# Moving the gather selections behind the column-tiled evictions, and trimming an image's last step

## The chip, the cores and the metric

The kernel runs on one core of a Trainium2 chip. Its engines work side by side, each through its own list of instructions in order: TensorE (PE) multiplies matrices into PSUM, VectorE (DVE) and ScalarE (ACT) do elementwise work and bring PSUM results to SBUF, GpSimd (POOL) mostly issues DMAs here, and SyncE (SP) issues some more. The metric is the time of one launch in microseconds (us), the median of several runs. Lower is better.

## The reference

The input is x of 8 images, 32 channels, 128 x 128 pixels, f32. After a group normalisation, layer 0 finds for each pixel the 8 best of 25 offsets in a 5 x 5 window (smallest sum of squared differences over a 3 x 3 patch and all channels) and gathers the 8 shifted copies into 256 channels, xb. Then:

```python
dct = _conv(xb, dct_w, groups=C)
h = jax.nn.relu(_conv(_conv(xb, w1), w2, groups=CK, pad=1))
h = jax.nn.relu(_conv(_conv(h, w3), w4, groups=CK, pad=1))
wiener = jax.nn.sigmoid(_conv(_conv(h, w5), w6, groups=CK, pad=1))
filt = _conv(wiener * dct, inv_dct_w, groups=C)
return _conv(filt, agg_w)
```

Each of w1, w3, w5 is a 1x1 convolution of 256 to 256 channels, and each of w2, w4, w6 a depthwise 3x3. The result is added to x. Layer 1 normalises again, applies one 5x5 kernel to all channels, and adds.

## The kernel before

**Steps and slots.** An image is cut into 16 blocks of 8 rows (NS = 16), and the main loop runs over 8 x 17 = 136 steps: the 17th step of an image (n == NS) only finishes the rows that still lack a neighbour below. Because each 3x3 convolution needs a row below, the second 1x1/3x3 pair works one row behind, the third two rows and the end three rows behind; so in the last step pair i has only i rows to give. Each step has four slots, for i in (3, 2, 1, 0). Slot i = 3, 2, 1 does the i-th pair of convolutions, for a block that is i - 1 steps old; slot 0 does the end (the DCT product, the aggregation) for a block two steps old. In each slot one unit (4 rows, 4 of the 8 copies) of a coming block is gathered.

**Two halves of the channels.** The upper 128 output channels of a pair go the V way: `pointwise_v` (L627 to L645) multiplies on PE into PSUM tiles pv, ACT copies them to tv, and `depthwise_v` (L674) starts the 3x3 with one ACT scale copy (L685), lets DVE add the other eight taps (L688), and ends with an activation on ACT ("dv", L692). The lower 128 go the T way: `pointwise_t` (L647) multiplies with the PE array split into four column groups of 32, so that the four groups hold the rows r, r + 4 of a block; the PSUM tile p holds them, ACT copies it to t (L667), and two DMAs on SP (L670, L672) bring the rows below and above into other partitions of t. `depthwise_t` (L696) does the 3x3 as matmuls from t into pw (L709), in a group of u = 0, 1, three dx and four j; with f32 each is two instructions, so 48 in a group. Two ACT activations (L721) bring pw to SBUF. The depthwise group of slot i is issued one slot later: "`next(dt)`", ahead of the gather in slot 0, behind it in the other slots. Its pw tiles have one buffer for each u.

**The gather.** `gather_load` (L548) issues on POOL the DMAs that bring pixel rows (xt) and, broadcast to all partitions, index rows (ib). `gather_select` (L578) makes on ACT, for each of two ib tiles, a Square with the partition's number as bias and a Relu (L584, L585), which leave 1 where the index fits and 0 elsewhere: the selection sel. `gather_pixels` (L588) multiplies xt with sel on PE (pg, L599), and ACT copies pg to xb (L606). In a slot, pixels of unit u, the selection of unit u + 1, and the load of unit u + 3 are issued.

**Work of the next image.** In between, the search for the best offsets of the next image and layer 1 of the last one are cut into small tasks that wait in four queues: "D" on DVE, "A" on ACT, "P" and "Q" on PE. A task has a cost in us, and may have a due time in ticks. `tick` (L886) grants each slot a credit, and runs D tasks for that credit. For the search a pair of difference tiles df is made on DVE (L410), squared on ACT at `run("A")` (L418), and summed on PE into pd at the next slot's `run("Q")` (L425). Other tasks transpose (px, pt, pi) or apply layer 1's 5x5 (p5, the line L836), at `run("P")`.

**What sets the order.** PE, DVE and ACT run in exactly the order of the program (`manual_schedule(engines=ORDERED)`). The DMA queues of POOL and SP are ordered by the framework. The PSUM tiles pv, p, pg, pc, pa, px, pt, pi, p5 share one pool ps_x of five buffers. In a slot the order is: pv and its copies, the scale copy; the last step's end (`later`, with pa); P tasks; in slot 0 the DCT product pc; Q tasks; the selection of u + 1 and the load of u + 3; the tick; DVE's taps; p with its copies to t; in slot 0 the depthwise group of slot 1; the pixels of u; in the other slots the depthwise group of the slot before; A tasks; then for the slot before dv and the activations of pw.

Of the kernel before, what the change touches and what calls it, by code (L numbers as in the profile page):

```python
# [17 lines left out]
C, K, H, W = 32, 8, 128, 128  # L18
CK = C * K
NO = 25  # L20
R = 8
NS = H // R
# [21 lines left out]
def bm3d_conv_preact(  # L44
# [16 lines left out]
    nc = tc.nc  # L61
# [85 lines left out]
    with tc.tile_pool(name="setup", bufs=1) as sp, tc.tile_pool(  # L147
# [23 lines left out]
        for name, w in (("w1", w1), ("w3", w3), ("w5", w5)):  # L171
            t = sp.tile([P, 2, CK], F32, name=f"nat_{name}", tag=f"nat_{name}")
            nc.sync.dma_start(t, w.rearrange("(m p) i a b -> p m (i a b)", p=P))
            if name == "w1":

                nat, t = t, sp.tile([P, 2, CK], F32, name="w1_kc")
# [6 lines left out]
        for name, dst in (("w1", lw1), ("w3", lw3), ("w5", lw5)):  # L183
            for g in range(2):
                ps = spp.tile([P, CK], F32, name=f"ps_{name}_{g}", tag="ps")
# [434 lines left out]
    def rows_before_v(i, b, n):  # L620
        v = tv[i - 1]
        if n < NS:
            nc.sync.dma_start(v[:, 0:2], v[:, R : R + 2])
        else:
            nc.gpsimd.memset(v[:, 0 : i + 1], 0.0)
# [21 lines left out]
    def pointwise_t(i, b, n, lhsT, src):  # L647
        t = tb[i - 1]
        nb = 2 if n < NS else 1
        if n == NS and i == 1:  # L650
            nc.gpsimd.memset(t[:, :, 2], 0.0)
        else:
            for q in range(2):
                ps = ps_x.tile([P, 2, 2, W], F32, name=f"p{i}_{b}_{n}_{q}", tag="x")
                for e in range(2):
                    s = slice(C * (2 * q + e), C * (2 * q + e + 1))
                    for g in range(2):
                        rows = src(g)
                        for r in range(4):
                            nc.tensor.matmul(  # L660
                                ps[C * r : C * (r + 1), e, :nb],
                                lhsT[:, g, s],
                                rows[:, r : r + 4 * nb - 3 : 4],
                                start=g == 0,
                                stop=g == 1,
                            )
                nc.scalar.copy(t[:, 2 * q : 2 * q + 2, 2 : 2 + nb], ps[:, :, :nb])  # L667
            for r in range(i - 1) if n == 0 else range(i - 1, 4) if n == NS else ():
                nc.gpsimd.memset(t[C * r : C * (r + 1), :, 2], 0.0)
        nc.sync.dma_start(t[64:P, :, 0:nb], t[0:64, :, 2 : 2 + nb])  # L670
        if nb == 2:
            nc.sync.dma_start(t[0:64, :, 1], t[64:P, :, 2])  # L672

    def depthwise_v(i, b, n):  # L674
        v = tv[i - 1]
        nr = R if n < NS else 4
        out_ = accp.tile([P, R, W], F32, name=f"acc{i}_{b}_{n}_1", tag=f"acc{i}1")
        acc = out_[:, :nr]
        for k, (dy, dx) in enumerate(
            ((1, 1), (0, 0), (0, 1), (0, 2), (1, 0), (1, 2), (2, 0), (2, 1), (2, 2))  # L680
        ):
            tap = dwv[:, i - 1, 3 * dy + dx : 3 * dy + dx + 1]
            rows = v[:, dy : dy + nr, dx : dx + W]
            if k == 0:
                nc.scalar.activation(acc, rows, AF.Copy, scale=tap)  # L685
                yield out_
            else:
                nc.vector.scalar_tensor_tensor(  # L688
                    acc, rows, tap, acc, op0=ALU.mult, op1=ALU.add
                )  # L690
        yield
        nc.scalar.activation(acc, acc, funcs[i - 1])  # L692
        yield
        rows_before_v(i, b, n)

    def depthwise_t(i, b, n):  # L696
        t = tb[i - 1].rearrange("p q (h k) w -> p q h k w", k=2)
        nb = 2 if n < NS else 1

        pt = [  # L700
            ps_dw.tile([P, 2, 2, W], F32, name=f"pw{i}_{b}_{n}_{u}", tag=f"dw{u}")
            for u in range(2)
        ]
        for u in range(2):
            hi = 96 if u == 0 else P
            for dx in (0, -1, 1):
                xa, xz = max(0, -dx), min(W, W - dx)
                for j in range(4):
                    nc.tensor.matmul(  # L709
                        pt[u][C * j : C * (j + 1), :, :nb, xa:xz],  # L710
                        dwd[0:hi, i - 1, u, j, dx + 1],
                        t[0:hi, j, :, :nb, xa + dx : xz + dx],
                        start=dx == 0,
                        stop=True,
                        skip_group_check=True,
                    )
        yield 1
        acc = accp.tile([P, R, W], F32, name=f"acc{i}_{b}_{n}_0", tag=f"acc{i}0")
        rows = acc.rearrange("p (k e) w -> p e k w", e=4)
        for u in range(2):  # L720
            nc.scalar.activation(rows[:, u:4:2, :nb], pt[u][:, :, :nb], funcs[i - 1])  # L721
        rows_before_t(i, b, n)
        accs[i, b, n][0] = acc

# [139 lines left out]
    lws, funcs = (lw1, lw3, lw5), (AF.Relu, AF.Relu, AF.Sigmoid)  # L864
    accs, fins = {}, {}

    def unit(stage, u):
        if 0 <= u < len(units) and units[u]:
            if stage is gather_load:
                at = (units[u][0], units[u][1] % 8 // 2)  # L870
                until(lambda: at in ready, 4.0)
            stage(*units[u])
# [28 lines left out]
    with tc.manual_schedule(engines=ORDERED):  # L901
        push(prep(0))
        push(mixes())
        xbd[0] = dram.tile([P, 2, H, W], F32, name="xbd_0", tag="xbd")
        for i in range(3):
            nc.gpsimd.memset(tb[i][0:64, :, 0], 0.0)
        for u in range(7):
            unit(gather_load, u)
            unit(gather_select, u - 2)
            unit(gather_pixels, u - 3)  # L910
        u = 4

        dt = dv = kept = iter(())

        later = lambda: None

        for s in range(len(steps) + 2):
            if s < len(steps):
                b, n = steps[s]
                if s == 2:  # L920
                    push(bands())
                if n == (0 if b else 4) and b + 1 < NB:
                    until(lambda: b in ready, 4.0)
                    push(prep(b + 1))
                if n == NS - 1 and b + 1 < NB:
                    until(lambda: b + 1 in ready, 4.0)
                    xbd[b + 1] = dram.tile([P, 2, H, W], F32, name=f"xbd_{b+1}", tag="xbd")
            for i in (3, 2, 1, 0):
                si = s - (i - 1 if i else 2)
                live = 0 <= si < len(steps)  # L930
                new_v = new_t = iter(())
                if live:
                    bi, ni = steps[si]

                if live and i:
                    src = source(i, bi, ni)
                    pointwise_v(i, bi, ni, lws[i - 1], src)
                    new_v, new_t = depthwise_v(i, bi, ni), depthwise_t(i, bi, ni)
                    accs[i, bi, ni] = [None, next(new_v)]
                later()  # L940
                later = lambda: None
                if live and not i:
                    if ni == 0:
                        x1d[bi] = dram.tile([C, H, W], F32, name=f"x1d_{bi}", tag="x1d")
                        stats[bi] = work.tile([P, NS + 1, 6], F32, name=f"stat_{bi}", tag="stat")
                    xr, xf, j0, j1 = fins.pop(si)
                run("P")
                if live and not i:
                    final_dct(bi, ni, accs[3, bi, ni], xf, j0, j1)

                run("Q")
                if s < len(steps):
                    unit(gather_select, u + 1)
                    unit(gather_load, u + 3)
                    tick(b, i)
                next(new_v, None)
                if live and i:
                    pointwise_t(i, bi, ni, lws[i - 1], src)
                next(kept, None)
                if not i:  # L960
                    next(dt, None)
                if s < len(steps):
                    unit(gather_pixels, u)
                    u += 1
                if i:
                    next(dt, None)
                run("A")
                next(dv, None)
                next(dt, None)
                kept, dv, dt = dv, new_v, new_t  # L970
                if live and not i:
                    later = partial(end, bi, ni, xr, j0, j1)
                if not i and 0 <= s - 1 < len(steps):
                    fins[s - 1] = final_load(*steps[s - 1])
        next(kept, None)
        later()
        until(lambda: NB - 1 in done, 4.0)
# [62 lines left out]
```

## Time and profile before

| | |
|---|---|
| median of 3 runs | 7131.84 us (7118.07 to 7140.6) |
| the profiled execution | 7131.18 us |
| its span, first to last instruction | 7129.4 us |
| mean granted clock of PE | 0.978 |
| PE busy | 6700.9 us, 94% |
| DVE busy | 5840.1 us, 82% |
| ACT busy | 5061.7 us, 71% |
| of it the selections (L584, L585) | 1165.4 + 1084.4 us, 1024 each |
| the t copies (L667) | 423.0 us, 800 |
| POOL busy | 2738.3 us, 38% |

Busy is the time in which an engine executes; the share is that of the span. A row of the waits reads: who waited, for whose result, total us, times, longest. A row of the timeline reads: start and length in us from the span's start, engine, line, operation, output and inputs, shapes, and how many instructions are merged; the bracket gives the idle time before it and what ended it. A row of the windows reads: the stretch, its length, then the busy us and instructions of PE, PE's weight loads, DVE, ACT and POOL, then PE's granted clock (1.00 is full), the DMA engines' share and GB/s. The clock row of the page gives the granted clock in tenths of full speed in 40 slices. PE's ends are modelled, so its busy time is an upper view.

### The profile page before, as it was taken

Reading aid. Unit: us, or ns where it says so; the run is one execution under the profiler, and the core shown is the slowest. Engines: PE = TensorE matmul, PEld = TensorE weight load, DVE = VectorE, ACT = ScalarE, POOL = GpSimd, SP = SyncE. Lnnn points to the kernel's source line nnn. Section 1 sums busy time; section 2 is a strip of 40 time slices with the busy share of each in tenths; the row PEclk is TensorE's granted clock in tenths of the full one; section 3 lists DMA queues with packets and bytes.
Section 4 is the critical chain, followed back from the end, with each engine's and each line's share of the span. In section 5 each row is a group of like instructions: output and inputs, shape, how many; then the busy total and the mean of one; then the engine's idle time right before and its main releaser. Section 6 shows DMA issues by size and latency. Waiting matters only on the chain. (4 is left out here: it accounts for less than half of the span.)

```text
span 7129.4 us, 229485 instructions
## 1 busy us (share of the span) xinstructions
PE 6700.9 (94%) x100226; PEld 3166.8 (44%) x100226; DVE 5840.1 (82%) x8606; ACT 5061.7 (71%) x6706; POOL 2738.3 (38%) x4599
## 2 busy tenths in 40 slices
PE   4699999999999999999999999999999999999997
PEld 1344444444444444444444444444444444444443
DVE  6689978888888898878888898888978889767675
ACT  4687768677686777867677776877768677666762
POOL 6244336333353343533335343543335333232222
PEclk8899999999999999999999999999999999999999
DMA  3566756666565575666656666566656666555652
GB/s 81 130 145 151 155 129 153 142 148 149 134 156 143 138 166 125 160 145 145 154 127 160 141 152 140 142 161 150 152 130 150 151 145 147 125 146 139 149 134 63
DMA packets 765484, 1007.70 MB, mean 141 GB/s; under 512 B 215008, under 2 KB 578592, under 8 KB 764480
## 3 DMA queue, kind: packets, MB, share of 16 engines
q0 software_dynamic: 378400, 733.67, 42.5%
q1 hardware_dynamic: 381056, 256.86, 17.0%
q8 instruction: 788, 12.91, 0.8%
q10 hardware_dynamic: 5024, 2.49, 0.2%
q14 instruction: 216, 1.77, 0.1%
HBM read 542.24 MB, written 217.01 MB: 106 GB/s over the span
## 5 line engine op out<-in xcount | busy, mean ns | idle before, releaser
L688 DVE SCALAR_TENSOR_TENSOR acc<-tv,dwv,acc 128x1024 f32<-128x1024 f32 (+1 forms) x3264 | 4084.0, 1253 | 223.1 <-ACT acc L685 109.5
L709 PE MATMUL pw<-t,dwd 128*32 128x508 f32 (+6 forms) x19584 | 2179.5, 592 | 156.8 <-DMA t<-t 109.4
L709 PEld LDWEIGHTS pw<-t,dwd 128*32 128x32 f32 (+1 forms) x19584 | 702.3, 111 | 1393.8 <-issue 1205.9
L570 POOL DMA_DIRECT2D ib<-idxd x1024 | 575.2, 563 | 1881.5 <-ACT sel L585 1764.8
L584 ACT ACTIVATE ib<-ib,nplace 128x1024 bf16<-128x1024 bf16 x1024 | 1165.4, 1138 | 25.6 <-DMA ib<-idxd 25.6
L585 ACT ACTIVATE sel<-ib 128x1024 f32<-128x1024 bf16 x1024 | 1084.4, 1059 | 32.6
L660 PE MATMUL p<-acc,lw 128*32 128x256 f32 x17408 | 994.1, 375 | 10.3 <-issue 10.0
L637 PE MATMUL pv<-acc,lw 128*128 128x512 f32 (+1 forms) x2112 | 971.9, 602 | 10.5 <-DVE acc L760 6.3
L606 ACT COPY xb<-pg 128x512 f32<-128x512 f32 x512 | 303.6, 593 | 713.5 <-PE pg L599 713.1
L645 ACT COPY tv<-pv 128x512 f32<-128x512 f32 (+2 forms) x784 | 444.8, 584 | 482.0 <-PE pv L637 463.6
L660 PEld LDWEIGHTS p<-acc,lw 128*32 128x32 f32 x17408 | 562.8, 110 | 429.6 <-issue 81.0
L721 ACT ACTIVATE acc<-pw 128x512 f32<-128x512 f32 (+1 forms) x816 | 452.8, 584 | 341.2 <-PE pw L709 340.8
L599 PEld LDWEIGHTS pg<-sel,xt 128*32 128x32 f32 x45056 | 591.2, 111 | 225.7 <-issue 126.1
L599 PE MATMUL pg<-sel,xt 128*32 128x48 f32 x45056 | 593.6, 206 | 82.9 <-issue 53.1
L780 DVE TENSOR_TENSOR xr<-xr,pa 128x256 f32<-128x256 f32 (+2 forms) x136 | 55.1, 405 | 717.9 <-PE pa L773 698.8
L637 PEld LDWEIGHTS pv<-acc,lw 128*128 128x128 f32 x2112 | 381.0, 191 | 407.7 <-issue 376.7
L410 DVE TENSOR_TENSOR df<-xn 128x786 f32<-128x786 f32 (+2 forms) x576 | 529.0, 969 | 17.2 <-PE pd L425 14.6
L667 ACT COPY t<-p 128x512 f32<-128x512 f32 x800 | 423.0, 570 | 119.8 <-PE p L660 116.5
L418 ACT ACTIVATE df<-df 128x786 f32<-128x786 f32 (+2 forms) x576 | 461.1, 862 | 50.4 <-DVE df L410 49.3
L685 ACT ACTIVATE acc<-tv,dwv 128x1024 f32<-128x1024 f32 (+1 forms) x408 | 459.8, 1127 | 45.8 <-PE pa L773 32.1
L637 PE MATMUL pv<-xb,lw 128*128 128x512 f32 x1024 | 475.7, 607 | 0.0
L757 PE MATMUL pc<-xf,ldct 128*128 128x512 f32 (+2 forms) x1056 | 470.9, 588 | 0.0
(128 smaller groups left out, 6397.3 us busy)
## 6 DMA issues: line engine op xcount, KB each, us to landing
ib<-idxd POOLq DMA_DIRECT2D x1024, 256.0 KB
xbd<-xb POOLq DMA_DIRECT2D x128, 1024.0 KB
xf<-xbd POOLq DMA_DIRECT2D x480, 256.0 KB
t<-t SPq DMA_DIRECT2D x792, 128.0 KB, 4.8
t<-t SPq DMA_DIRECT2D x384, 256.0 KB, 4.9
tv<-tv SPq DMA_DIRECT2D x384, 130.0 KB, 4.1
xt<-xtd POOLq DMA_DIRECT2D x240, 176.0 KB
xl<-xs POOLq DMA_DIRECT2D x256, 64.0 KB
```

The source lines that it names most:

```text
L410: nc.vector.tensor_sub(df[:, :, ca:cz], xn[:, r0 : r0 + SR, ca:cz], xn[:, r0 + dy : r0 + dy + SR, ca + dx : cz + dx],)
L418: nc.scalar.activation(df[:, :, ca:cz], df[:, :, ca:cz], AF.Square)
L570: nc.gpsimd.dma_start(ib.rearrange("p k y x -> p (k y x)"), idxd[b][s4 // 8, s4 % 8, 4 * k0 : 4 * k0 + 8] .rearrange("k x -> (k x)") .part ...
L584: nc.scalar.activation(ib, ib, AF.Square, bias=nplace)
L585: nc.scalar.activation(sel, ib, AF.Relu, scale=-1.0, bias=1.0)
L599: nc.tensor.matmul(pg[C * j : C * (j + 1), :, xa:xz], xt[:, t], sels[j // 2][:, j % 2, :, xa:xz], start=True, stop=True,)
L637: nc.tensor.matmul(ps[:, :hr], lhsT[:, g, P:CK], src(g)[:, h : h + hr], start=g == 0, stop=g == 1,)
L660: nc.tensor.matmul(ps[C * r : C * (r + 1), e, :nb], lhsT[:, g, s], rows[:, r : r + 4 * nb - 3 : 4], start=g == 0, stop=g == 1,)
L685: nc.scalar.activation(acc, rows, AF.Copy, scale=tap)
L688: nc.vector.scalar_tensor_tensor(acc, rows, tap, acc, op0=ALU.mult, op1=ALU.add)
L709: nc.tensor.matmul(pt[u][C * j : C * (j + 1), :, :nb, xa:xz], dwd[0:hi, i - 1, u, j, dx + 1], t[0:hi, j, :, :nb, xa + dx : xz + dx], start ...
L757: nc.tensor.matmul(ps[:, : z - a], ldct[:, m], xf[:, m, a:z], start=True, stop=True)
```

## The change

Two things are done. First, in the main loop `gather_select` of unit u + 1 and `gather_load` of unit u + 3 move from ahead of the tick to behind `gather_pixels` of unit u. On ACT the selections thus stand behind the copies to t and the copy to xb, and ahead of the A tasks, dv and the activations of pw. The load's DMAs on POOL move behind those of the tick.

Second, in an image's last step (n == NS) `pointwise_t` multiplies and copies only i - 1 rows where it did 4 (for i = 1 it did none already), `depthwise_v` works on i rows where it did 4, and `depthwise_t` on as many rows of each u as lie among the i that count: 1 and 0 for i = 1, 1 and 1 for i = 2, 2 and 1 for i = 3, where it did 2 and 2.

```diff
 def pointwise_t(i, b, n, lhsT, src):
+        nr = 4 if n < NS else i - 1
-                        for r in range(4):
+                        for r in range(nr):
...
-                nc.scalar.copy(t[:, 2 * q : 2 * q + 2, 2 : 2 + nb], ps[:, :, :nb])
+                nc.scalar.copy(
+                    t[: C * nr, 2 * q : 2 * q + 2, 2 : 2 + nb], ps[: C * nr, :, :nb]
+                )
 def depthwise_v(i, b, n):
-        nr = R if n < NS else 4
+        nr = R if n < NS else i
 def depthwise_t(i, b, n):
+        nh = [2 if n < NS else (i + 1 - u) // 2 for u in range(2)]
-                for j in range(4):
+                for j in range(4 if nh[u] else 0):
                     nc.tensor.matmul(
-                        pt[u][C * j : C * (j + 1), :, :nb, xa:xz],
+                        pt[u][C * j : C * (j + 1), : nh[u], :nb, xa:xz],
                         dwd[0:hi, i - 1, u, j, dx + 1],
-                        t[0:hi, j, :, :nb, xa + dx : xz + dx],
+                        t[0:hi, j, : nh[u], :nb, xa + dx : xz + dx],
...
-            nc.scalar.activation(rows[:, u:4:2, :nb], pt[u][:, :, :nb], funcs[i - 1])
+            if nh[u]:
+                nc.scalar.activation(
+                    rows[:, u : u + 2 * nh[u] - 1 : 2, :nb], pt[u][:, : nh[u], :nb], funcs[i - 1]
+                )
 main loop, each slot
                 run("Q")
                 if s < len(steps):
-                    unit(gather_select, u + 1)
-                    unit(gather_load, u + 3)
                     tick(b, i)
...
                 if s < len(steps):
                     unit(gather_pixels, u)
+                    unit(gather_select, u + 1)
+                    unit(gather_load, u + 3)
                     u += 1
                 if i:
                     next(dt, None)
                 run("A")
```

## The prediction

> **What bounds the kernel now.** I read the page first, for the engines' totals and the clock row. TensorE (PE) is busy 94% of the span and no other engine comes near it:
>
> ```profile
> PE 6700.9 (94%) x100226; PEld 3166.8 (44%) x100226; DVE 5840.1 (82%) x8606; ACT 5061.7 (71%) x6706; POOL 2738.3 (38%) x4599
> PEclk8899999999999999999999999999999999999999
> ```
>
> The question is therefore which waits are left on PE, and what else could put new ones there. Second view, PE's waits:
>
> ```profile
> PE pw L709 <- DMA t<-t: 109.4, 53, 12.1
> PE pg L599 <- issue: 53.1, 36, 4.7
> ...
> PE pd L425 <- ACT df L418: 29.5, 29, 2.9
> PE pw L709 <- issue: 27.2, 16, 5.4
> ```
>
> Of some 430 us idle (span less busy) a good part lies before 300 us, in the start. In the body the largest single wait is the depthwise matmuls (pw) waiting for the row copies of t. Third view, ScalarE's (ACT) waits: it has much idle time, and most of it is spent before the pixel copy xb.
>
> ```profile
> ACT xb L606 <- PE pg L599: 713.1, 179, 13.4
> ACT tv L645 <- PE pv L637: 463.6, 439, 3.2
> ```
>
> Fourth view, the timeline of ACT and then PE in one ordinary slot (i = 2, behind slot 3):
>
> ```profile
> 3109.81 0.59 ACT L606 COPY xb<-pg 128x512 f32<-128x512 f32 x1 [0.33 <-PE pg L599]
> 3110.29 1.60 ACT L418 ACTIVATE df<-df 128x786 f32<-128x786 f32 x2
> 3111.79 0.57 ACT L645 COPY tv<-pv 128x512 f32<-128x512 f32 x1
> 3113.40 0.59 ACT L645 COPY tv<-pv 128x512 f32<-128x512 f32 x1 [1.04 <-PE pv L637]
> 3114.02 1.15 ACT L685 ACTIVATE acc<-tv,dwv 128x1024 f32<-128x1024 f32 x1
> 3115.08 1.13 ACT L584 ACTIVATE ib<-ib,nplace 128x1024 bf16<-128x1024 bf16 x1
> 3116.24 1.06 ACT L585 ACTIVATE sel<-ib 128x1024 f32<-128x1024 bf16 x1
> 3117.21 1.13 ACT L584 ACTIVATE ib<-ib,nplace 128x1024 bf16<-128x1024 bf16 x1
> 3118.37 1.06 ACT L585 ACTIVATE sel<-ib 128x1024 f32<-128x1024 bf16 x1
> 3119.34 1.05 ACT L667 COPY t<-p 128x512 f32<-128x512 f32 x2
> ```
>
> ```profile
> 3109.66 3.70 PE L637 MATMUL pv<-acc,lw 128*128 128x512 f32 x8
> 3113.30 0.86 PE L425 MATMUL pd<-df,neg 128*32 128x393 f32 x8
> 3113.98 3.63 PE L660 MATMUL p<-acc,lw 128*32 128x256 f32 x64
> ...
> 3118.80 1.49 PE L709 MATMUL pw<-t,dwd 96*32 96x512 f32 x12 [0.28 <-DMA t<-t]
> ```
>
> Two things are to be seen. PE finished p at 3117.6, but its eviction to t starts only at 3119.34, behind four selection instructions that take 3119.34 - 3115.08 = 4.26 us. And the squares of df run right behind xb and end at 3111.9, 1.4 us before PE wants them for pd at 3113.30. The first is what the moved block relieves. The second is what it is put in front of.
>
> Last, the windows view shows what a PE wait costs beyond itself: the stretch from 3087.50 to 3091.00 follows a 2.29 us wait for t, and its granted clock is 0.56.
>
> ```profile
> 3087.50:3091.00 3.50, 3.45 (x20) 1.25 (x24) 3.36 (x18) 0.00 (x0) 1.31 (x2) 0.56 0.07 20
> 3091.00:3094.50 3.50, 3.50 (x45) 1.22 (x40) 0.05 (x1) 0.00 (x0) 0.89 (x2) 0.95 0.32 86
> ```
>
> The 48 matmuls there spread over 7.03 us against 5.33 elsewhere: 1.70 us more, half of a 3.41 us stretch at half clock. In the body (300 to 7040 us) half-clock stretches followed 1 of 59 PE waits under 1.6 us, 7 of 24 between 1.6 and 2.2, 16 of 25 between 2.2 and 3, and 11 of 11 above 3.
>
> **The change part by part.** The sum is made against the profiled execution: 7131.18 us, a span of 7129.4 and 1.8 around it; the median of the runs is 7131.84, so either may stand as base.
>
> *t earlier (gain).* With the selections gone from before them, the t copies start as soon as p and the scale copy (L685) are done. By the timeline, the end of p to the end of t is usually 3.0 to 3.4 us; without the queue about 1. I went through the depthwise groups that waited after 300 us: 122.5 us of first waits, and of each I count no more than what its t copy lay behind p less 1.0 us. That gives 97 us; the rest are waits that the earlier copy doesn't reach. In 24 of these groups the half clock cost a further 46 us, of which I take 38. Bounds: nothing, if the landing is set by shared DMA queues (from 2.4 to 14.2 us, median 4.9), to all 168. SP's order stays; each t copy's two DMAs only start earlier on it.
>
> *Squares later (loss).* Behind xb the order becomes selections, squares, dv activation, pw evictions, and next slot's pv copies. In the slot shown: pg's end 3109.66, first selection 0.63 later, 4.26 of selections, 1.60 of squares, and about 0.45 for the second half of pd: pd would end 6.98 us behind pg where it ended 4.5. PE loses 2.5 us. The same step for all 184 places where squares follow an xb copy (0.75 us per further square, so that four squares end 8.0 us behind pg): between slots 3 and 2 PE has only pv before pd, and 31 of 42 are late, 58 us in all; between slots 0 and 3 it has pv and pa, 47 of 66 are late, 89 us; where a 5.33 us depthwise group lies between, 6 of 76, 2 us. Sum 150 us. It can be half, if PE would have waited there for something else; nothing in the wait table is large enough to absorb all.
>
> *Clock (loss).* The delays counted are 32 under 1.6 us, 15 up to 2.2, 31 up to 3 and 6 above. By the shares above, 15 x 7/24 + 31 x 16/25 + 6 = 30 half-clock stretches of 1.71 us: 52 us. Bounds 0 to 84 x 1.71 = 144. The Trainium skill, "TensorE: Matmul & The Clock Gate" (the section on HAM oscillation), asks only that PE have no gaps above about 3.4 us; by that rule nearly all of these delays would be free of a clock loss, and the sum below would come out about 50 us lower. The trace disagrees: 23 of its 49 body waits between 1.6 and 3 us were followed by half clock, so the row decides.
>
> *PSUM buffers (loss).* ps_x has five buffers, and pv of slot 3 is now evicted some 7.4 us behind pg(0): 0.66 + 4.26 + 0.95 (dv) + 0.95 (pw) + 0.6. In 7 slots 3 with pi and no pd, PE wants the first one back at 3.7 + 1.07 + 0.4 = 5.2 us: 2.2 x 7 = 15 us. Elsewhere p or p5 fills the time. Bounds 0 to 30.
>
> *Short slots (loss).* A selection is now done 4.92 us behind pg, and the next pg wants it. Ordinary slots have pv 3.70 and p 3.66 between. At an image's end slot 2 has pv of 0.7 and p of 1.95, slot 3 pv 1.13, pa 1.07, p 1.9: 2.0 and 0.8 us missing, once per image, less some waits already there: 20 us. Bounds 0 to 25.
>
> *VectorE (loss).* Taps of slot 3 wait for a scale copy now 9.0 us behind pg(0); DVE otherwise gets there at about 7.7. DVE has 699 us idle waiting for pa, which covers it except in the steps full of max searches: 10 us, bounds 0 to 40. If that cover were gone it would be 1.3 us in each of 136 steps, 177.
>
> *Gather loads (0).* POOL's ib load is freed by the selection and so starts later, but is wanted two slots later: about 15 us, as before. POOL's work of the tick now stands ahead of it. POOL already waits 1764.8 us for sel in front of ib, so its rank matters little. ACT waited 25.6 us for ib; bounds -25 to 25.
>
> *Last step.* A short depthwise group takes 2.79 us (48 matmuls of 256 columns). Rows left: half of the columns and half of the groups for i = 1 (0.7 us), half the columns for i = 2 (1.4), three quarters for i = 3 (2.1): 4.2 us an image, 33 us gained, bounds 15 to 33. pointwise_t issues 16 or 32 instead of 64, but the four row groups ran side by side, so their time is that of one group: 16 x 0.11 = 1.8 us, nothing gained. A single row may lose the overlap of weight loads: the nearest row is pc at 128 columns, 5.1 us for 32, 0.16 each, so +0.8 us in 8 slots: 6 us, bounds 0 to 13. VectorE's eight taps shrink from 0.75 us each, covered by the same 699 us idle; ACT's two activations likewise, by its 713 us before xb.
>
> Sum: 150 + 52 + 15 + 20 + 10 + 6 = 253 lost, 97 + 38 + 33 = 168 gained, +85: 7131 + 85 = **7216 us**.
>
> **Rivals.**
> - *Shared queues set the landing:* t copies earlier, waits unchanged, gains 33 only: +220, 7351. For: the waits with 8 to 14 us from t to pw lie where POOL's large loads run. Against: the ones with 5.4 us, and ib loads now come behind t.
> - *Late ACT was behind the unexplained waits too (faster):* if the waits under "issue" at pg and pw (53.1 + 27.2, with about 12 half-clock stretches, 20 us) are unseen waits for ACT, they go, and all 168 of t: 253 - 33 - 168 - 100 = -48, 7083. With all of t's 168 gone the balance is still +52, so 73 of the other 100 us must go to pass 7110. Against: such waits lie in the middle of a pg group.
> - *The loss is absorbed:* no half clock and no PSUM or DVE delay: 253 - 52 - 15 - 10 = 176 against 168: 7139, no change. PE then waits in two short pieces at pd, since its first half needs only the first square.
>
> **How the numbers follow.** A measurement here tells about 0.3% (21 us) from no change. Likeliest 0.48; shared queues 0.17; unexplained waits 0.21; absorbed 0.14, of which 0.09 within 0.3%, 0.04 slower, 0.01 faster. Slower 0.69, same 0.09, faster 0.22. The likeliest alone spans 7150 to 7290; the bounds of clock and squares with the rivals make 7070 to 7350 for 8 in 10.
>
> **What would show it.** Waits of pw on t<-t fall from 109 to below 30; pd on df rises from 29.5 to about 170; xb's idle grows; the mean clock stays near 0.98; pw's matmul time falls by some 33. It is wrong if pd's wait stays under 80, or t's stays above 80.

## The result, and the profile after

The changed kernel takes 7226.48 us (median of 4 runs, 7215.5 to 7247.15) against 7136.22 before in the same company: a ratio of 1.0133, with a 95% interval of 1.0101 to 1.0166. It is slower by 1.3%. The profiled execution took 7218.32 us, 87 more than the one before (7131.18); the prediction said 85 more.

The totals and the clock row of the page of the changed kernel:

```profile
PE 6739.9 (93%) x99394; PEld 3155.5 (44%) x99394; DVE 5792.3 (80%) x8606; ACT 5053.7 (70%) x6698; POOL 2729.2 (38%) x4599
PEclk8799999999999999999999999999999999999998
```

PE has 832 matmul instructions fewer and yet is busy 39 us longer, because a group whose inputs come one after the other is stretched (the 2304 matmuls of pd are busy 387 us where they were 301), and matmuls at half clock take longer. The waits of PE, of ACT and of DVE in the changed kernel (who waited for what, total us, times, longest):

```profile
PE pd L425 <- ACT df L418: 142.3, 102, 3.1
PE pi L534 <- DVE o L525: 75.0, 16, 19.9
PE pg L599 <- ACT sel L585: 34.9, 19, 10.8
PE pw L714 <- DMA t<-t: 31.2, 15, 5.5
...
PE pw L714 <- ACT acc L727: 10.2, 19, 1.2
```

```profile
ACT xb L606 <- PE pg L599: 1123.8, 401, 16.1
ACT t L668 <- PE p L661: 401.1, 356, 5.1
```

```profile
DVE xr L788 <- PE pa L781: 600.0, 115, 9.6
DVE acc L691 <- ACT acc L688: 282.1, 127, 7.6
```

The two rows that the change was about moved the way that was foretold, if not quite as far: the wait for t fell from 109.4 to 31.2 us, and the wait for the squares rose from 29.5 to 142.3. ACT's idle time before xb rose by 411 us, some 320 of it in slot 0, where the selection had been filling it. DVE waits 282 us for its scale copy, where the kernel before has this:

```profile
DVE acc L688 <- ACT acc L685: 109.5, 97, 5.8
```

The timeline of one slot 2 of the changed kernel, ACT's lines and then PE's, shows the new wait at work. Between the pixels and the squares stand the four selections; PE has finished pv and sits 2.10 us in front of pd.

```profile
3163.35 1.15 ACT L584 ACTIVATE ib<-ib,nplace 128x1024 bf16<-128x1024 bf16 x1
...
3166.66 1.06 ACT L585 ACTIVATE sel<-ib 128x1024 f32<-128x1024 bf16 x1
3167.63 1.59 ACT L418 ACTIVATE df<-df 128x786 f32<-128x786 f32 x2
3169.12 1.05 ACT L645 COPY tv<-pv 128x512 f32<-128x512 f32 x2
```

```profile
3163.26 3.17 PE L637 MATMUL pv<-acc,lw 128*128 128x512 f32 x7
3168.52 1.27 PE L425 MATMUL pd<-df,neg 128*32 128x393 f32 x6 [2.10 <-ACT df L418]
```

### The profile page after: what moved, and what is told of

The parts are those of the page before. It is cut to its first block, busy times and chain, and to the rows that moved or that the text cites. A ratio compares the mean times of both kernels' runs of the same rounds, so it can differ in the third digit from the quotient of the medians.

```text
span 7216.2 us, 227868 instructions
## 1 busy us (share of the span) xinstructions
PE 6739.9 (93%) x99394; PEld 3155.5 (44%) x99394; DVE 5792.3 (80%) x8606; ACT 5053.7 (70%) x6698; POOL 2729.2 (38%) x4599
## 5 line engine op out<-in xcount | busy, mean ns | idle before, releaser
L691 DVE SCALAR_TENSOR_TENSOR acc<-tv,dwv,acc 128x1024 f32<-128x1024 f32 (+3 forms) x3264 | 4030.9, 1237 | 395.5 <-ACT acc L688 282.1
L714 PE MATMUL pw<-t,dwd 96*32 96x508 f32 (+6 forms) x19392 | 2125.2, 586 | 70.3 <-DMA t<-t 31.2
L714 PEld LDWEIGHTS pw<-t,dwd 96*32 96x32 f32 (+1 forms) x19392 | 674.5, 111 | 1284.5 <-issue 1217.3
L584 ACT ACTIVATE ib<-ib,nplace 128x1024 bf16<-128x1024 bf16 x1024 | 1170.6, 1143 | 19.3 <-DMA ib<-idxd 19.3
L606 ACT COPY xb<-pg 128x512 f32<-128x512 f32 x512 | 301.0, 588 | 1124.3 <-PE pg L599 1123.8
L661 PE MATMUL p<-acc,lw 128*32 128x256 f32 x16768 | 1029.4, 380 | 6.5 <-issue 5.5
L668 ACT COPY t<-p 128x512 f32<-128x512 f32 x800 | 444.8, 578 | 411.4 <-PE p L661 401.1
L599 PE MATMUL pg<-sel,xt 128*32 128x48 f32 x45056 | 619.0, 206 | 76.2 <-ACT sel L585 34.9
L410 DVE TENSOR_TENSOR df<-xn 128x786 f32<-128x786 f32 (+2 forms) x576 | 529.2, 967 | 60.5 <-PE pd L425 54.6
L645 ACT COPY tv<-pv 128x512 f32<-128x512 f32 (+2 forms) x784 | 426.3, 578 | 179.3 <-PE pv L637 172.6
L425 PE MATMUL pd<-df,neg 128*32 128x390 f32 (+2 forms) x2304 | 387.2, 537 | 150.9 <-ACT df L418 142.3
L727 ACT ACTIVATE acc<-pw 128x512 f32<-128x512 f32 (+2 forms) x808 | 423.5, 568 | 103.6 <-PE pw L714 103.5
L752 POOL DMA_DIRECT2D xf<-xbd x544 | 340.0, 632 | 363.5 <-PE pc L765 343.0
```

The source lines that it names most:

```text
L410: nc.vector.tensor_sub(df[:, :, ca:cz], xn[:, r0 : r0 + SR, ca:cz], xn[:, r0 + dy : r0 + dy + SR, ca + dx : cz + dx],)
L425: nc.tensor.matmul(pd[C * j : C * (j + 1), :, ca:cz], neg[:, 28 - 4 * aa[e] : 60 - 4 * aa[e]], df[:, SR // 2 * h : SR // 2 * (h + 1), ca:c ...
L584: nc.scalar.activation(ib, ib, AF.Square, bias=nplace)
L599: nc.tensor.matmul(pg[C * j : C * (j + 1), :, xa:xz], xt[:, t], sels[j // 2][:, j % 2, :, xa:xz], start=True, stop=True,)
L661: nc.tensor.matmul(ps[C * r : C * (r + 1), e, :nb], lhsT[:, g, s], rows[:, r : r + 4 * nb - 3 : 4], start=g == 0, stop=g == 1,)
L668: nc.scalar.copy(t[: C * nr, 2 * q : 2 * q + 2, 2 : 2 + nb], ps[: C * nr, :, :nb])
```

## The experiments

Ratios are to the kernel before, run beside each kernel; medians of the kernel before lay between 7133 and 7149 us from chip to chip, so kernels of different groups are best compared by ratio.

| kernel | median us | ratio, 95% interval |
|---|---|---|
| changed | 7226 | 1.0133 (1.0101 to 1.0166) |
| block moved, last step untrimmed | 7224 | 1.0113 (1.0094 to 1.0132) |
| last step trimmed alone | 7153 | 1.0021 (1.0010 to 1.0033) |
| squares ahead of the selections | 7181 | 1.0063 (1.0041 to 1.0085) |
| selections between t and xb | 7074 | 0.9910 (0.9891 to 0.9928) |
| slot 0's selection at its old place | 7133 | 0.9976 (0.9963 to 0.9990) |
| pd behind p | 7099 | 0.9932 (0.9908 to 0.9956) |
| selections split around t | 7058 | 0.9875 (0.9850 to 0.9901) |
| split, last step trimmed | 7028 | 0.9831 (0.9799 to 0.9862) |
| squares ahead, slot 0 as before | 7045 | 0.9882 (0.9862 to 0.9902) |
| split, half behind xb | 7067 | 0.9910 (0.9891 to 0.9929) |
| split and trimmed, pd behind p | 7024 | 0.9851 (0.9832 to 0.9871) |

### The two parts, each alone

The block moved, with the last step as before:

```diff
                 if s < len(steps):
-                    unit(gather_select, u + 1)
-                    unit(gather_load, u + 3)
                     tick(b, i)
...
                     unit(gather_pixels, u)
+                    unit(gather_select, u + 1)
+                    unit(gather_load, u + 3)
                     u += 1
```

> The moved block alone, the last step as before. If the terms of the sum hold (the last step's rows worth 33 us on PE less 6 for lone rows), this is 27 us slower than the changed kernel: about 7253 us, with pd's wait for the squares at 140 us as there. If the trimmed rows are hidden behind other waits, it is the same as the changed kernel, 7226.

The last step alone keeps the other lines of the diff: `nr`, `nh` and the slices by them.

> The last step's rows alone, the selections where they were. If the sum holds, 27 us faster than before: about 7109 us, the waits for t near 109 us and the squares' near 30 as before. If the last step is not set by PE, 7136.

The block alone is 1.0113 and the changed kernel 1.0133, so within the intervals all of the loss is in the move, and the trimmed rows gain nothing there. Alone they even cost 0.2%. Yet the work they take away is exactly what was counted. The short depthwise matmuls by shape, first before, then trimmed alone (busy us and mean ns of one behind the bar):

```profile
L709 PE MATMUL pw<-t,dwd 128*32 128x254 f32 x384 | 26.1, 386 | 0.0
L709 PE MATMUL pw<-t,dwd 96*32 96x254 f32 x384 | 26.0, 384 | 0.0
L709 PE MATMUL pw<-t,dwd 128*32 128x256 f32 x192 | 15.8, 390 | 0.0
L709 PE MATMUL pw<-t,dwd 96*32 96x256 f32 x192 | 15.3, 388 | 3.6 <-DMA t<-t 3.6
```

```profile
L714 PE MATMUL pw<-t,dwd 128*32 128x127 f32 x256 | 10.7, 281 | 0.0
L714 PE MATMUL pw<-t,dwd 96*32 96x127 f32 x256 | 10.1, 272 | 0.0
L714 PE MATMUL pw<-t,dwd 96*32 96x254 f32 x128 | 9.4, 409 | 0.0
L714 PE MATMUL pw<-t,dwd 128*32 128x128 f32 x128 | 7.2, 283 | 0.1
L714 PE MATMUL pw<-t,dwd 96*32 96x128 f32 x128 | 6.8, 282 | 0.0
...
L714 PE MATMUL pw<-t,dwd 96*32 96x256 f32 x64 | 5.6, 417 | 3.4 <-DMA t<-t 3.4
```

83.2 us became 49.8: 33 us saved, as predicted. Two of the three steps in which an image's short groups fall (those of i = 2 and i = 3) show where they went. One such stretch of the same two steps, in the windows view, before and then trimmed alone (length; PE, weight loads, DVE, ACT, POOL busy; granted clock; DMA):

```profile
1917.00:2013.00 96.00, 86.02 (x1545) 46.99 (x1544) 84.09 (x92) 80.93 (x114) 49.30 (x79) 1.00 0.54 139
```

```profile
1928.00:2031.00 103.00, 89.86 (x1481) 46.87 (x1480) 80.97 (x92) 80.63 (x115) 45.42 (x76) 0.92 0.56 136
```

PE issues 64 matmuls fewer and is busy 4 us longer, at a granted clock of 0.92 instead of 1.00. Over the seven stretches of this kind the sum is 682 us before and 697 trimmed. In them, time at half clock grew from 48 to 102 us, which costs about 27 us, and PE's idle time from 69 to 83 us. So what the rows freed here was lost again to idle time and to the clock; that the gaps brought the half clock is read from the trace, not tested. This is one profiled execution of each, and as a whole the trimmed one was 3 us the shorter (7128.28 against 7131.18). But it was the fastest of seven; their median is 13 us longer, and all seven had a mean clock of 0.972 to 0.975, where the kernel before had 0.975 to 0.979 beside them.

### Squares ahead of the selections

```diff
                     unit(gather_pixels, u)
-                    unit(gather_select, u + 1)
-                    unit(gather_load, u + 3)
                     u += 1
                 if i:
                     next(dt, None)
                 run("A")
+                if s < len(steps):
+                    unit(gather_select, u)
+                    unit(gather_load, u + 2)
```

> The changed kernel with the selections one place further back, behind the squares (A tasks) instead of ahead of them; ahead of dv, of the pw evictions and of the next slot's pv copies as in the changed kernel. Theory 1 (the loss is the squares' lateness): the 190 us by which pd ended later and the half clock behind it go, the t copies stay early: about 7010 us, 6980 to 7060, pd's wait below 20. Theory 2 (the loss is what the selections hold up in the next slot: pv's eviction, the scale copy, VectorE's taps, the five PSUM buffers): still about 7200, with the wait for pd replaced by others.

It is 7181 us, near theory 2. The wait for the squares is back where it was before the change (28.9 against 29.5 us), and others stand in its place. PE, ACT and DVE in this kernel:

```profile
PE pg L599 <- ACT sel L585: 59.5, 31, 10.5
PE pg L599 <- ACT tv L645: 35.2, 33, 2.3
PE pw L714 <- ACT acc L727: 33.5, 22, 3.2
...
PE pd L425 <- ACT df L418: 28.9, 26, 2.9
...
PE p L661 <- ACT tv L645: 19.5, 14, 2.2
```

```profile
ACT df L418 <- DVE df L410: 121.5, 77, 5.0
```

```profile
DVE acc L691 <- ACT acc L688: 338.3, 118, 7.7
```

pg and p wait for the evictions of pv (the five buffers), pw for its own, and pg for the selection. The row of ACT has grown: the squares wait for DVE's difference tiles, 121.5 us against 24.0 in the changed kernel, and the selections are queued behind that wait. Part of it is only that the squares come earlier again, for the kernel before has this:

```profile
ACT df L418 <- DVE df L410: 49.3, 27, 4.1
```

### Selections between the t copies and xb

```diff
                 if s < len(steps):
+                    unit(gather_select, u + 1)
+                    unit(gather_load, u + 3)
                     unit(gather_pixels, u)
-                    unit(gather_select, u + 1)
-                    unit(gather_load, u + 3)
                     u += 1
```

> The changed kernel with the selections between the t copies and the pixel copy xb: the t copies are early as in the changed kernel, the squares where they were before. Both theories of the loss: about 6975 us (7136 less 135 for t's waits and their half clock, less 27 for the last step), 6950 to 7020. If the waits for t are set by the shared DMA queues and not by the t copies, 7110, with the waits for t near 100 us.

7074 us, the first kernel faster than before, though 100 us above the expectation. PE's two rows and ACT's:

```profile
PE pd L425 <- ACT df L418: 75.6, 53, 2.9
...
PE pw L714 <- DMA t<-t: 23.1, 11, 4.2
```

```profile
ACT t L668 <- PE p L661: 698.7, 573, 5.4
```

The wait for t is gone as far as in the changed kernel, so it is the t copies that set it and not the queues. But the expectation that the squares would be where they were was wrong: ACT now idles 699 us for p, ahead of the selections, where before it made selections in that time and idled 116.5; so xb and the squares come later, and pd's wait is 75.6 us instead of 29.5.

### Selections split around the t copies

This follows from the last row: 699 us over the 400 slots with t copies is 1.7 us a slot, so half a selection (2.13 us) about fits in the time in which ACT waits for p.

```diff
-                    unit(gather_select, u + 1)
-                    unit(gather_load, u + 3)
+                    unit(select_0, u + 1)
                     tick(b, i)
...
                 if s < len(steps):
+                    unit(select_1, u + 1)
+                    unit(gather_load, u + 3)
                     unit(gather_pixels, u)
```

Here `select_0` and `select_1` are `gather_select` for the first and the second ib tile.

> The kernel before, with only the second half of each selection (the second ib tile, 2.13 us) moved behind the t copies, still ahead of xb; the first half stays where it was, in the time in which ScalarE waits for p. The t copies can then start when p ends, and xb, the squares, dv and the next slot come when they came before. If what t's lateness costs is the 135 us of the sum (97 of waits, 38 of half clock), and the loss of the changed kernel is all due to what the selections push back: about 7005 us, 6985 to 7060, below the 7074 of the selections wholly between t and xb, pd's wait near 30. If t's lateness costs little and something else made that kernel fast, about 7074 or more.

> The same with the trimmed last step. By the sum 27 us below the split alone. By what the trimmed rows alone showed (0.2% slower, their 33 us of matmuls gone, but half clock in the steps at an image's end), 0 to 15 us above it.

7058 and, trimmed, 7028 us: the lowest so far, 1.25 and 1.7% below the kernel before. In the trimmed one the waits of PE are:

```profile
PE pd L425 <- ACT df L418: 44.9, 35, 2.9
PE pw L714 <- DMA t<-t: 35.8, 23, 3.8
```

The gain of an early t, with little else late (pd's wait is 37.0 us in the untrimmed split), is thus 1.25%, 90 us of the 135 expected. Trimmed, the kernel is 30 us faster, about the 27 of the sum, though the two intervals overlap. In the profiled executions only 18 us of the difference lie in the three steps with short groups; 19 lie in a step of the next image, where no row was cut and less time ran at half clock. With the selections where they were, and in the changed order, the rows made those three steps 2 and 4 us longer. The clock falls here too, from 0.96 to 1.00 in the untrimmed split's image-end stretches to 0.95 to 0.98. So the trimmed rows are worth something in this order, but hardly shown to be worth 30 us; why the order matters was not tried.

### Slot 0 alone, and pd behind p

```diff
+                    if not i:
+                        unit(gather_select, u + 1)
+                        unit(gather_load, u + 3)
                     tick(b, i)
...
                     unit(gather_pixels, u)
-                    unit(gather_select, u + 1)
-                    unit(gather_load, u + 3)
+                    if i:
+                        unit(gather_select, u + 1)
+                        unit(gather_load, u + 3)
```

> The changed kernel with the selection of slot 0 back at its old place, in the long wait of ScalarE for the pixels of that slot; the other three slots as changed. Theory 1 (squares late): of 190 us by which pd ended later, the 115 between slots 0 and 3 go, with their share of half clock: about 7226 - 140 = 7085, pd's wait near 60. Theory 2 (ScalarE as a whole late after pg, the wait moves on to pv's eviction once the squares are in time): slot 0 is where ScalarE has most to do before pv, so most of that goes too: below 7085, 7050 to 7085. If the slots weigh alike, a quarter of 90 to 130 us: 7195.

```diff
-                run("Q")
...
                     pointwise_t(i, bi, ni, lws[i - 1], src)
+                run("Q")
```

> The changed kernel with TensorE's sum of the squares (pd) issued behind p instead of ahead of it, so that it wants the squares 3.7 us later; ScalarE's order untouched but for sm. Theory 1: the lateness of up to 2.9 us goes wherever one pair is squared: about 7226 - 190 - 30 = 7010, pd's wait below 20. Theory 2: TensorE runs into the wait behind it, for pv's eviction and the five buffers, as it did with the squares put first (7181): 7150 to 7190, with p, pg and pv waiting for tv 50 to 100 us in all.

Slot 0 alone gives back 1.0133 - 0.9976 = 1.6%, 112 us, more than the whole net loss; the four slots do not weigh alike. PE and ACT with slot 0 as before:

```profile
PE pd L425 <- ACT df L418: 92.3, 56, 2.9
```

```profile
ACT xb L606 <- PE pg L599: 665.8, 470, 13.1
```

pd's wait falls by 50 us, and ACT's idle time before xb from 1123.8 to 665.8 us. Counted over the same 184 places as in the prediction, the 115 us by which pd ended later between slots 0 and 3 fall to 3, while the 73 between slots 3 and 2 stay, at 75: so the 115 did go, as theory 1 says, and 112 us came back. What did not go is the half clock that was to make it 140: it takes 154 us of the body, against 150 in the changed kernel.

With pd behind p the time is 0.9932: 2.0%, 143 us given back, between the two theories' numbers (7010, and 7150 to 7190). PE and DVE:

```profile
PE pd L425 <- ACT df L418: 37.1, 33, 2.9
PE p L661 <- ACT tv L645: 32.4, 14, 4.2
...
PE pg L599 <- ACT tv L645: 17.4, 21, 1.4
```

```profile
DVE df L410 <- PE pd L425: 109.0, 42, 4.3
```

So both theories hold in part. Against the split, the block moved alone loses 1.0113 - 0.9875 = 2.4%, 170 us, and 143 come back when pd hardly waits for the squares any more, so most of the loss is the squares. With these out of the way, PE runs into pv's eviction (50 us), and DVE waits 109 us for pd to free its difference tiles, where it waited 54.6 in the changed kernel.

### Squares ahead, with slot 0 as before

> The squares put ahead of the selections as in the run before of that kind (7181), and slot 0's selection at its old place. Theory 3 (there the gain was lost because the squares wait for VectorE's difference tiles, 121 us, with the selections queued behind that wait; VectorE was late because slot 0's selection delays the scale copy of slot 3): with slot 0 as before, ScalarE's wait for the difference tiles falls to about 50 us, VectorE's for the scale copy from 338 to about 150, and the time to about 7060, below slot 0 alone (7133) by its remaining 69 us of pd waits. Against it, theory 4 (selections ahead of dv, the pw evictions and pv cost by themselves in every slot): 7110 to 7140, with the waits for tv and for pw's buffers staying at 50 us and more.

The edit is that of the squares ahead of the selections and that of slot 0 together. It takes 7045 us, 15 below the number of theory 3 and far below that of theory 4. ACT and DVE:

```profile
ACT df L418 <- DVE df L410: 69.9, 48, 4.1
```

```profile
DVE acc L691 <- ACT acc L688: 155.2, 125, 7.9
```

The chain that the rows show is: slot 0's selection late on ACT, so slot 3's scale copy late, so DVE late with its taps and the next difference tiles, so the squares wait for DVE, and what stands behind them waits too. Taking slot 0 out shortens both waits, and the time goes from 7181 to 7045, 1.8% by the ratios. The wait of pw for its eviction stays (34.6 us against 33.5), the one part of theory 4 that held.

But that this chain ate the gain of the squares is not shown. Four kernels make a square: slot 0 put back gives 1.6% with the squares behind the selections and 1.8% with them ahead; the squares put ahead give 0.7% with slot 0 moved and 0.9% with slot 0 as before. Within the intervals the two remedies just add. So slot 0's selection costs about the same whether the squares or something else stands behind it, and the squares put ahead did help, by 50 and 67 us, though far less than the 185 and 127 us by which pd, place by place, then ends earlier.

### Two more on the split

```diff
                 if s < len(steps):
-                    unit(select_1, u + 1)
-                    unit(gather_load, u + 3)
                     unit(gather_pixels, u)
+                    unit(select_1, u + 1)
+                    unit(gather_load, u + 3)
                     u += 1
```

> The split selections with trimmed last step (7028), the second half one place further back: behind xb instead of ahead of it. By the timeline xb is then copied 2.1 us earlier in slots 1 to 3, but the squares, dv, pw and pv come no later than they did, since t, xb and the half selection only change places. If only the lateness of the squares and of what follows them counts: 7028, within 20. In slot 0 the half is now behind the pixels, 2.13 us of ScalarE's work that was hidden: by half of slot 0's 95 us (7226 less 7133), 45 us more: 7070. This tells whether slot 0 costs by itself, without a whole selection being late elsewhere.

7067 us, near the number given for slot 0's cost. ACT and PE:

```profile
ACT xb L606 <- PE pg L599: 906.9, 243, 13.6
```

```profile
PE pd L425 <- ACT df L418: 67.3, 48, 2.9
```

ACT's idle time before xb was 605 us, and of the 302 more 240 lie in slot 0; pd's wait was 44.9. But place by place, pd ends 32 us later than in the split between slots 3 and 2, where the expectation had nothing later, and only 10 between slots 0 and 3. Whether slot 0's lateness is carried on into slot 3, or the half selection of slot 3 costs by itself, was not tried. So half a selection behind the pixels of every slot costs 0.8%; that this is slot 0's cost is not shown, and the right number may be luck.

> The split selections with trimmed last step (7028), and pd issued behind p. If pd's 45 us of waits and their half clock are the next thing on TensorE: 6975 to 7000. If VectorE's difference tiles, which wait for pd to free their buffers (109 us where pd was put behind p in the changed kernel, 28 before), take it back: 7020 to 7050.

0.9851 against 0.9831: no gain, the second of the two outcomes. pd's wait falls from 44.9 to 25.6 us, and DVE's wait for pd to free the difference tiles rises from 23.5 to 66.8, which fits that VectorE takes it back:

```profile
DVE df L410 <- PE pd L425: 66.8, 22, 4.3
```

(The 28 us of the expectation are this row with the last step trimmed alone, 27.7; in the kernel before it is 14.6.)

## Why the prediction was right, and where it was not

The direction, the size and the main mechanism held. That the size is right to 10 us is partly luck, for the terms were off and offset each other. The early t was put at 135 us and gave 90 in the split. The losses of the move were put at 247 us, and the block moved alone lost 170 against the split. The trimmed rows were put at 27 us and gave nothing in this order. So the gains were some 70 us too large and the losses nearly 80.

- *t earlier*: 97 us of waits predicted, the row fell by 78. By the split kernel it is worth 90 us in time, where waits and clock together were put at 135. The term was some 45 us too large, or a little less, as the squares are not quite in time there.
- *Squares later*: 150 us predicted. By the same count over the same 184 places, pd ends 190 us later in all: 73 between slots 3 and 2, 115 between 0 and 3, 2 elsewhere. The step's working was short by the tail: pd ends 7.3 us behind pg where 6.98 was worked out (its four parts add to 6.94), and about 9 for four squares where 8.0 was. Not all of the 190 us is lost time, for the whole loss of the move is 170. The wait row, 142.3, missed the 170 foretold; part of the lateness lies inside the groups of pd, whose busy time rose from 301 to 387 us.
- *Clock*: 52 lost and 38 gained, 14 net. Half-clock stretches in the body were 36 where they had been 35, 150 us long in all against 154. They moved from pw to p, as PE now loses the clock at pd. The balance is 16 us better than predicted; the two halves were not seen apart.
- *PSUM buffers*: 15 us predicted, hardly a wait in the changed kernel (0.7 us of p for tv). The wait at pd hides it, and it shows once pd is out of the way (50 us with pd behind p).
- *Short slots*: 20 us predicted; pg's wait for sel rose by 16.
- *VectorE*: 10 us predicted, with the cover named: the wait for pa. It gave 99 us (698.8 to 600.0) of the 173 by which the wait for the scale copy grew. The rest comes out, among other places, as pi waiting for o, 42.7 to 75.0. By that row the term was some 20 us too small, perhaps more.
- *Gather loads*: nothing predicted; ACT's wait for ib is 19.3 us against 25.6.
- *Last step*: the matmuls saved are the 33 us of the step, and lone rows of p cost none of the 6 us (35.4 against 35.1 us). But the time did not follow: of the terms, this is the one that failed outright. "33 us gained" took PE's work for the kernel's time, at a place where PE is not dense (613 of 682 us busy in the seven stretches).
- The first step began 10 us later than before (its pa at 357.0 against 346.9 us), and at 356 to 357 us in all four kernels that move the whole selection of every slot behind the pixels. In the other kernels it began at 349 to 355, so not all of the 10 us need be the move's. No term stood for it, and its cause was not tried.

Of the rivals, shared queues fell with the t copies' wait, the absorbed loss fell with the 1.3%, and the unexplained waits stayed in good part (pg 30.9 and pw 22.8 us of 53.1 and 27.2). What the kernel before wasted on t was real, and so was the way to get it without the loss: put behind t only as much of the selection as ACT would otherwise have spent waiting.

## What to carry to other kernels

When a block moves back in an engine's list, write down what stood behind its new place and when each of those is wanted; here the squares were wanted first, the pv evictions and the scale copy next, and removing one wait brought out the next. Look at the idle time that the block used to fill: the 4.3 us of a selection were free in slot 0 and about half of them beside p, and a block can be cut to fit such a gap. When two remedies are tried together, run all four kernels: here they added, where a chain between them had been supposed. Work saved on the busiest engine need not come out as time where that engine has gaps.

## What the runs showed that was not expected

Fewer matmuls can go with a lower granted clock: at an image's end the kernel with the last step trimmed alone ran at 0.90 to 0.96 in all seven stretches, where the one before had 0.97 to 1.00 in five of them, and took 697 instead of 682 us. And the changed kernel lost the clock as the one before did, behind other waits: 16 of its 45 PE waits between 1.6 and 3 us were followed by half clock (23 of 49 before), none of those below 1.6. Half-clock stretches followed waits of pw 25 times and of pd once in the kernel before, and 12 times each in the changed one.
